# A PixArt-style block on one core: bias rows on GpSimd's queue, a LayerNorm moved into the stage before, and a new order in the last slots of self-attention

## The chip, the cores and the metric

The kernel runs on one core of a Trainium2 chip, in float32 throughout. A core has five engines with a queue each: TensorE (PE in the profile; its weight loads are listed as PEld), VectorE (DVE), ScalarE (ACT), GpSimd (POOL) and SyncE (SP). SP, ACT and POOL also issue transfers (DMAs) between the chip's main memory, called DRAM in the code, and the core's own memories SBUF and PSUM. An engine works through its queue in order; an instruction that waits holds up all that stand behind it on that engine. The metric is the device time of one execution in microseconds (us); lower is better.

## The reference

`x` is 8 sequences of 512 tokens with 512 channels, the context is 8 times 77 tokens, the condition one vector per sequence. There are 16 heads of 32 channels. Four stages follow each other, each adding to `x`:

```python
# 1 cross attention with adaptive LayerNorm on both sides ("x")
ada = lambda x, W, b: (1 + scale) * ln(x) + bias      # scale, bias = split(silu(c) @ W + b)
q  = ada(x, Wss_q, bss_q) @ Wq + bq
kv = ada(context, Wss_kv, bss_kv) @ Wkv + bkv
x  = x + softmax(q @ k.T / sqrt(32)) @ v @ Wp + bp
# six vectors for the later stages: shift_a, scale_a, gate_a, shift_m, scale_m, gate_m
mods = split(silu(c) @ W_mod + b_mod, 6)
# 2 self attention ("a")
x = x + gate_a * (attention((1 + scale_a) * ln(x) + shift_a) @ W_proj + b_proj)
# 3 cross attention with plain LayerNorm ("c")
x = x + (attention(ln(x) @ W_qc + b_qc, ln(context) @ W_kvc + b_kvc) @ W_cproj + b_cproj)
# 4 MLP ("m")
x = x + gate_m * (gelu(((1 + scale_m) * ln(x) + shift_m) @ W_mlp1 + b_mlp1) @ W_mlp2 + b_mlp2)
```

## The kernel before

The kernel works batch by batch (one sequence of 512 tokens as four tiles of 128) and stage by stage; between stages `x` goes through DRAM tensors `xa`, `xc`, `xm`. A batch's sequence is one SBUF tile of 1 MB, and three such tiles exist (`xres`). Weights pass through five SBUF tiles of 1 MB (`weights`).

**Setup (lines 228 to 262).** ACT's queue issues the loads of the condition (`c_sb`), of the context (`cx`, two transfers), and of nine bias vectors into the rows of one tile `brow` (line 237); then ACT computes `cs`, the Silu of the condition. PE transposes `brow` into `bcol`, which holds every bias as a column, and `cs` into `csT`. `mod_pair` (line 168) then computes scale and bias of the adaptive LayerNorm, for the context (`mod_kv`) and for `x` (`mod_q`): for each half it loads a weight, multiplies (line 175), copies the result out on ACT (line 180), transposes it back (line 183) and adds the bias on DVE (line 187).

**Context (`context_x`, line 401).** DVE normalises the five row tiles of the context, PE transposes them channel block by channel block (`cT_ps_x`, line 420), DVE multiplies by the scale (line 424) and adds the bias (line 428). Then come the values (line 394; they go through DRAM to be laid out by token) and the keys (line 442).

**Cross phase (`cross_phase`, line 528; used for x and c).** It runs over 32 units (batch b, head group fc). A unit has `scores` (PE line 561, then the softmax on DVE and ACT, lines 570 to 579), and `outputs` of the unit before (transposes line 597, copies on ACT, products line 602, `oT` on DVE line 609). In between, a queue of small generators (`Filler`) supplies matmuls: the queries of the next unit, the projection of the batch before (`project`, residual on DVE line 352 and POOL line 356, store line 357), and the LayerNorm of the next batch (`ln_T`, line 303): statistics on DVE (line 274), a reciprocal root in twelve small DVE steps (lines 286 to 295), `xh` (line 299), transposes (line 315). `next_x` loads the sequence of the next batch on ACT's queue at the first unit of each batch. The order of PE is the program's; DVE, ACT, POOL and SP are ordered by the compiler's list scheduler, which follows its own estimate of when each instruction is ready. `issue_after(ins)` forces what its block issues on the engine of `ins` to stand behind `ins` in that engine's queue; the dictionary `behind` hands such instructions to `ln_T`.

**Self phase (`self_phase`, line 650).** Here all five engines follow the order of the program. A group is one head group of one batch, and each slot of the loop (line 911) finishes group g and starts the next: scores of the next group (line 771) are copied to `e` on ACT (line 789) while DVE takes maxima (line 791); `maxima` and `spread` (lines 803, 806, 814, 820) write the row maxima to DRAM; `shift` (line 825) adds their negatives to `e` by eight accumulating transfers on POOL's queue; then come the exponentials (line 834), sums (line 841), outputs (line 854), the total (line 864) and the division (lines 871, 874). `beside` gives each slot its matmul work (values, queries, keys, projections). `later` keeps the residual additions and stores of projections, which `flush` issues. In the last batch, `ContextC` loads, normalises and transposes the context for stage c. After the loop the last group is finished together with the context's values (line 394) and keys (line 518): this is called the last slot. The slot (7,1) below is the one of batch 7, head group 1.

## Time and profile before

| what | value |
|---|---|
| time of the runs, median of 3 | 2706.99 us (2702.71 to 2710.66) |
| the profiled execution: its own time, and its span from first to last instruction | 2709.26 us, 2707.5 us |
| PE, DVE, ACT, POOL busy, share of the span | 95%, 62%, 39%, 30% |
| granted PE clock, mean over the span | 0.983 |
| first scores of stage x; last projection of stage x starts | 85.9 us; 494.5 us, 14 us long |
| first transposes of stage a; first scores of stage c | 515.5 us; 1499.3 us |
| last store of stage c's result | 1899.6 us |

In the profile, "L12" is line 12 of the kernel before. A timeline line has the start in us, the length in us, the engine, the line, the operation, output and inputs, shapes, a count, and in square brackets how long the engine was idle before and what released it. "ACTq" and "SPq" are the queues' own transfer issues. A line of the list of waits has the engine, its line, what it waited for, then the total in us, how often, and the longest. The first letters of a tile's name are sometimes cut by the profile, and the releaser of a wait on several transfers is the one that came last by its records.

### The profile page before, as it was taken

The page shows a single profiled execution, that of the slowest core. Times are in us where ns is not written, and L with a number is a line of the kernel's source. Part 1 is how long each engine was busy: PE and PEld are TensorE (multiplying, and loading weights), DVE is VectorE, ACT ScalarE, POOL GpSimd, SP SyncE. Part 2 cuts the span into 40 slices and gives each one's busy share as a digit, 9 for nine tenths or more (in the row PEclk, how much of TensorE's full clock was granted, in tenths as well). Part 3 has the DMA queues.
Part 4 walks back from the last instruction along what each step waited for, and adds up shares of the span by engine and source line. Part 5 has one row for each costly group of instructions (what it writes and reads, how often), then busy time and mean ns, then how long its engine had stood idle before and what let it go on. Part 6 is the DMA issues. An engine that isn't in the chain of part 4 may idle for free. (4 is left out here: it accounts for less than half of the span.)

```text
span 2707.5 us, 33555 instructions
## 1 busy us (share of the span) xinstructions
PE 2562.5 (95%) x13029; PEld 1498.7 (55%) x13029; DVE 1677.8 (62%) x2917; ACT 1058.7 (39%) x1466; POOL 822.0 (30%) x679
## 2 busy tenths in 40 slices
PE   6999999889999999999988999999999999999998
PEld 2555554433333333333333544454788888888887
DVE  4666666456776766767573767776755455465553
ACT  1433333256666666665752433333211211211210
POOL 0000001146766767667673001011411011011011
PEclk9989999999999999999999999999999999999999
DMA  6111121268988898998887111113110111110110
GB/s 243 40 51 51 48 82 52 82 125 176 178 182 184 180 186 168 195 184 175 178 194 209 58 36 43 47 40 105 51 35 29 39 36 34 34 35 34 34 36 24
DMA packets 114757, 264.95 MB, mean 98 GB/s; under 512 B 10418, under 2 KB 27406, under 8 KB 114598
## 3 DMA queue, kind: packets, MB, share of 16 engines
q0 software_dynamic: 36864, 134.23, 26.1%
q1 hardware_dynamic: 58037, 90.54, 10.0%
q10 hardware_dynamic: 19697, 38.03, 4.4%
q8 instruction: 103, 1.69, 0.2%
q14 instruction: 56, 0.46, 0.1%
HBM read 226.39 MB, written 36.37 MB: 97 GB/s over the span
## 5 line engine op out<-in xcount | busy, mean ns | idle before, releaser
L789 ACT COPY e_a<-sT_a 128x1024 f32<-128x1024 f32 x256 | 253.7, 1013 | 137.5 <-PE sT_a L771 109.9
L834 ACT ACTIVATE e_a<-e_a 128x1024 f32<-128x1024 f32 x256 | 262.7, 1056 | 49.8 <-DMA e_a<-mxd_a 47.1
L1244 POOL TENSOR_TENSOR res_m<-res_m,gate_m 128x256 f32<-128x256 f32 x64 | 52.1, 814 | 665.1 <-DVE res_m L1242 665.1
L825 POOL DMA_DIRECT2D e_a<-mxd_a x256 | 228.1, 2056 | 77.8 <-DMA mxd_a<-mxT_a 46.9
L791 DVE TENSOR_TENSOR mx_a<-sT_a,mx_a 128x1024 f32<-128x1024 f32 x128 | 152.8, 1220 | 123.9 <-PE sT_a L771 103.8
L841 POOL TENSOR_TENSOR sum_a<-e_a,e_a 128x1024 f32<-128x1024 f32 x64 | 152.4, 2400 | 195.1 <-ACT e_a L834 195.1
L1178 ACT ACTIVATE hT<-hT,bcol 128x512 f32<-128x512 f32 x128 | 91.9, 722 | 236.7 <-DVE hT L1153 228.6
L356 POOL TENSOR_TENSOR x_x<-x_x,res_x 128x512 f32<-128x512 f32 x32 | 40.5, 1266 | 468.8 <-DVE res_x L352 396.5
L771 PE MATMUL sT_a<-qT_a,kT_a 32*128 32x512 f32 x1024 | 149.2, 647 | 13.4 <-ACT e_a L789 12.6
L854 PE MATMUL o_ps_a<-e_a,v 128*32 128x512 f32 x1024 | 147.6, 617 | 11.4 <-ACT e_a L834 11.2
L841 POOL TENSOR_TENSOR sum_a<-sum_a,e_a 128x1024 f32<-128x1024 f32 x64 | 149.8, 2363 | 12.8 <-ACT e_a L834 12.5
L356 POOL TENSOR_TENSOR x_c<-x_c,res_c 128x512 f32<-128x512 f32 x32 | 40.6, 1270 | 369.2 <-DVE res_c L352 296.3
L598 ACT COPY pT_x<-pT_ps_x 77x512 f32<-77x512 f32 x128 | 73.0, 577 | 167.0 <-PE pT_ps_x L597 165.1
L329 PE MATMUL q_ps_x<-xnT_x,w_L_xcond_Wq 128*128 128x512 f32 x256 | 134.8, 613 | 0.0
L871 DVE RECIPROCAL rz_a<-z_ps_a 128x512 f32<-128x512 f32 x32 | 107.3, 3353 | 43.6 <-PE z_ps_a L864 43.6
L841 DVE TENSOR_TENSOR sum_a<-sum_a,e_a 128x1024 f32<-128x1024 f32 x64 | 86.3, 1379 | 75.4 <-ACT e_a L834 50.1
L1145 PE MATMUL q_ps_h<-x_m,w_L_xcond_W_mlp 128*128 128x256 f32 x512 | 132.3, 381 | 0.0
L329 PE MATMUL q_ps_c<-xnT_c,w_L_xcond_W_qc 128*128 128x512 f32 x256 | 131.6, 600 | 0.0
L1145 PE MATMUL q_ps_h<-xT_m,w_L_xcond_W_mlp 128*128 128x256 f32 x512 | 131.4, 379 | 0.0
L1145 PE MATMUL q_ps_h<-x_m,w_s 128*128 128x256 f32 x512 | 122.1, 382 | 5.6 <-DVE w_s L1099 4.6
L337 PE MATMUL proj_ps_x<-w_L_xcond_Wp,oT_x 128*128 128x512 f32 x256 | 123.4, 626 | 3.4 <-DVE oT_x L609 3.4
L598 ACT COPY pT_c<-pT_ps_c 77x512 f32<-77x512 f32 x128 | 72.3, 577 | 128.7 <-PE pT_ps_c L597 128.7
(236 smaller groups left out, 5110.0 us busy)
## 6 DMA issues: line engine op xcount, KB each, us to landing
e_a<-mxd_a POOLq DMA_DIRECT2D x256, 512.0 KB, 14.9
x_x<-in_x_dram ACTq DMA_DIRECT2D x8, 1024.0 KB, 5.0
xa<-x_x SPq DMA_DIRECT2D x32, 256.0 KB, 2.0
x_a<-xa ACTq DMA_DIRECT2D x8, 1024.0 KB
xr_a<-xa ACTq DMA_DIRECT2D x32, 256.0 KB, 7.7
xc<-xr_a SPq DMA_DIRECT2D x32, 256.0 KB, 2.1
x_c<-xc ACTq DMA_DIRECT2D x8, 1024.0 KB, 5.1
w_L_xcond_W_mlp<-in_L_xcond_W_mlp_dram SPq DMA_DIRECT2D x8, 1024.0 KB, 5.2
```

The lines of the kernel that those rows point to most:

```text
L329: nc.tensor.matmul(ps, lhsT=w[:, k, ts(j, P)], rhs=xT[k], start=(k == 0), stop=(k == KC - 1))
L337: nc.tensor.matmul(ps, lhsT=xT[k][:, cols], rhs=w[:, k, :], start=(k == 0), stop=(k == KC - 1))
L598: nc.scalar.copy(pTs[-1][:, h % 2, :], pp[:S, :])
L771: nc.tensor.matmul(sc[h // 2][:, h % 2, :], lhsT=kT[ts(h, HD), ts(k, P)], rhs=qT[ts(h, HD), :], start=True, stop=True,)
L789: nc.scalar.copy(self.e[k][i], sc[i])
L791: nc.vector.tensor_tensor(self.mx[1 - i], sc[1 - i], self.e[0][1 - i] if k == 1 else self.mx[1 - i], ALU.max,)
L825: nc.gpsimd.dma_start(out=self.e[k][i].rearrange("p h n -> p (h n)"), in_=self.mxd[2 * i : 2 * i + 2, :] .rearrange("h n -> (h n)").partit ...
L834: nc.scalar.activation(self.e[k][i], self.e[k][i], AF.Exp)
L841: engine.tensor_tensor(sum_i, self.e[0][i] if k == 1 else sum_i, self.e[k][i], ALU.add)
L854: nc.tensor.matmul(self.po[ts(h, HD), :], lhsT=vt[:, self.fc * P + h * HD : self.fc * P + (h + 1) * HD], rhs=self.e[k][h // 2][:, h % 2, : ...
L871: nc.vector.reciprocal(r, self.pz)
L1145: nc.tensor.matmul(self.banks[n][:, half], lhsT=lhsT, rhs=rhs, start=(k == 0), stop=(k == len(pairs) - 1),)
```

## The change

It has parts at four places.

1. *Setup and context.* The nine bias rows are issued by GpSimd's queue. `csT` is made before `bcol`. `mod_pair` becomes `mod_half`, which takes an already loaded weight and gives back its ACT copy; the two halves for the context stay in the setup, the two for `x` go into `context_x`, one after every second channel block. The weights are loaded in another order. The load of the first sequence is queued behind the last ACT copy of the context's modulation. The bias addition of the context (four times) moves from DVE to GpSimd. The PSUM pools `ps_s` and `ps_x` get the finer setting by which a tile waits only for the tiles of an earlier pool that it overlaps.
2. *Cross phases.* The statistics of batch 0 are queued on DVE behind the context's last multiplication (x) or, as before, behind the last division of self (c); those of batch 1 behind the softmax of unit (0,0), which held for c alone before; those of batch b+2 behind the softmax of unit (b,2). Each sequence's load is queued on ACT behind the last exponential of the unit before.
3. *From x to self.* The first LayerNorm of the self phase (`normalise_a(0)`) is written into the end of stage x, before the last `outputs`.
4. *The end of self.* All four shifts of a slot are written at its start, which leaves each engine's own order as it was. In batch 7, slot (7,1) has its queries and keys first and only one projection, slot (7,2) has three; the context for c is loaded in (7,1) instead of (7,2), and its LayerNorm is cut into other pieces, the reciprocal root after the `maxima`. In the last slot the copies of the context's values (evacuations) are issued one step later, after the next exponential and addition, and the loads of the first sequence of c and of the residual tiles go from ACT's queue to SP's.

```diff
-    def mod_pair(wname, bname, dst, pool, psp):
-        for u in range(2):
-            w = load_w(wname, u)
-            ps = psp.tile([P, H], F32, tag="ps", name=f"mod_ps_{wname}_{u}")
...
+    def mod_half(u, w, bname, dst, pool, psp, tag):
+        ps = psp.tile([P, H], F32, tag=tag, name=f"mod_ps_{bname}_{u}")
...
+        mark = nc.scalar.copy(m, ps[:B, :])
...
+        return mark
...
-    def next_x():
+    def next_x(queue=nc.scalar):
...
-            nc.scalar.dma_start(
+            nc.gpsimd.dma_start(
                 out=brow[at : at + n, :],
...
         nc.scalar.activation(cs, c_sb, AF.Silu)
+        cp = spp.tile([P, H], F32, tag="ps", name="csT_ps")
+        for k in range(KC):
+            nc.tensor.transpose(cp[:, ts(k, B)], cs[:, ts(k, P)], ident[:B, :B])
+        nc.vector.tensor_copy(csT.rearrange("p k b -> p (k b)"), cp[:, : KC * B])
         bp = spp.tile([P, H], F32, tag="ps", name="bcol_ps")
...
-        mod_pair("L0_xcond_Wss_kv", "L0_xcond_bss_kv", mod_kv, sp, spp)
-        w_l0 = [load_w("L0_xcond_Wkv", 0), load_w("L0_xcond_Wkv", 1)]
-        mod_pair("L0_xcond_Wss_q", "L0_xcond_bss_q", mod_q, sp, spp)
-        next_x()
+        w_ss_kv = [load_w("L0_xcond_Wss_kv", u) for u in range(2)]
+        for u in range(2):
+            mark = mod_half(u, w_ss_kv[u], "L0_xcond_bss_kv", mod_kv, sp, spp, "ps")
+        w_ss_q = [load_w("L0_xcond_Wss_q", 0)]
+        w_l0 = [None, load_w("L0_xcond_Wkv", 1)]
+        w_l0[0] = load_w("L0_xcond_Wkv", 0)
+        w_ss_q.append(load_w("L0_xcond_Wss_q", 1))
+        with tc.issue_after(mark.ins):
+            next_x()
...
+    def normalise_a(b):
+        xb = [x_sb["a", 0][:, t, :] for t in range(NT)]
+        mv, y = yield from ln_stats_pieces(xb, P, 1e-6, f"a{b}")
+        yield
+        for t in range(NT):
+            normalise(xb[t], xb[t], mv, y, t, P)
+            if t % 2:
+                yield
...
-    with tc.tile_pool(name="ps_s", bufs=2, space=PSUM) as ps_s:
+    with tc.tile_pool(name="ps_s", bufs=2, space=PSUM, reuse_waits="tile") as ps_s:
...
+            yield
             v = v()
             nc.scalar.copy(v[:n, :], pv[:n, :])
...
-                nc.vector.tensor_tensor(
+                last = nc.vector.tensor_tensor(
                     d, pt[:, :R].rearrange("p (b s) -> p b s", s=S),
...
-                nc.vector.tensor_tensor(
+                nc.gpsimd.tensor_tensor(
                     d, d, mod_kv[:, KC + k, :].unsqueeze(2).to_broadcast([P, B, S]), ALU.add
                 )
+                if k % 2:
+                    mark = mod_half(k // 2, w_ss_q[k // 2], "L0_xcond_bss_q", mod_q, prep, ps_m, "m")
...
-                    if t == CT // 2:
+                    if t in (2, CT - 1):
                         yield
                 y = rsqrt(mv[:, :, 1], 1e-6, "cc", CT)
...
-                    nc.scalar.activation(p, p, AF.Exp)
+                    behind["load"] = nc.scalar.activation(p, p, AF.Exp)
...
-                if behind:
+                if fc == 0:
                     behind.setdefault(1, last)
+                elif fc == 2:
+                    behind.setdefault(b + 2, last)
...
                         b, eps, nm, work, ps_m, st[b]["xT"], mod_q[:, 0:KC, :], mod_q[:, KC:, :],
+                        behind=behind.get(b),
...
                 if fc == 0:
-                    next_x()
+                    with tc.issue_after(behind["load"].ins):
+                        next_x()
...
+                elif fc == 1 and not more:
+                    todo = [queries(b, 3), keys(b, 3), project(b - 1, 0)]
+                elif fc == 2 and not more:
+                    todo = [project(b - 1, t) for t in (1, 2, 3)]
...
-            run(ln_pieces(0))
             for k in range(KC):
                 transpose_x(0, k)
...
+                for k in range(NT):
+                    g.shift(k)
+                flush(0)
                 flush(1)
...
-                if not more and fc == 2:
-                    ctx_c.load()
-                    ln = ctx_c.norm()
-                g.shift(0)
-                g.shift(1)
...
                 nxt.scores(1)
...
+                if fc == 2 and not more:
+                    next(ln, None)
                 g.exp(0)
                 pump(f[1], 4)
+                if fc == 1 and not more:
+                    ctx_c.load()
+                    ln = ctx_c.norm()
...
                 nxt.scores(3)
-                if fc == 2 and not more:
-                    next(ln, None)
...
                 nxt.maxima()
-                if fc == 0 and more:
+                if fc == 0 and more or fc == 2 and not more:
                     next(ln, None)
...
                 if fc == 2 and not more:
-                    next(ln, None)
+                    for _ in ln:
+                        pass
                 g.add_up(3)
...
+            value = None
             for k in range(NT):
                 g.exp(k)
                 if k:
                     g.add_up(k)
+                    run(value)
                 g.outputs(k)
+                if k == 2:
+                    next_x(nc.sync)
+                    for t in range(NT):
+                        load_tile(B - 1, t, nc.sync)
                 if k + 2 < CT:
-                    ctx_c.values(k + 2)
-                if k == 2:
-                    next_x()
-                    for t in range(NT):
-                        load_tile(B - 1, t)
+                    value = ctx_c.values(k + 2)
+                    next(value)
+            run(value)
...
             behind = {0: g.finish()}
-            run(ctx_c.keys(1))
+            behind["load"] = run(ctx_c.keys(1))
...
-            ps_m = stack.enter_context(tc.tile_pool(name="ps_x", bufs=2, space=PSUM))
+            ps_m = stack.enter_context(tc.tile_pool(name="ps_x", bufs=2, space=PSUM, reuse_waits="tile"))
...
             cross_phase(
-                "x", 1e-5, w_l0[2:], names, True, kT, vs, stack, between=later_modulation
+                "x", 1e-5, w_l0[2:], names, True, kT, vs, stack, behind={0: last, "load": mark},
+                between=later_modulation, ending=lambda: run(normalise_a(0)),
             )
```

## The prediction

> **What bounds the kernel now.** I read the page first, then TensorE's waits, then the timeline at the four places where the long waits lie. On the page TensorE (PE) is the bound: 95% busy, DVE 62%, ACT 39%. So only PE's idle stretches can be won, and each must be found by its place. The waits of PE, longest in total first:
>
> ```profile
> PE 2562.5 (95%) x13029; PEld 1498.7 (55%) x13029; DVE 1677.8 (62%) x2917; ACT 1058.7 (39%) x1466; POOL 822.0 (30%) x679
> ...
> PE bcol_ps L245 <- DMA row_L_xcond_b_mod<-in_L_xcond_b_mod_dram: 17.4, 1, 17.4
> ...
> PE o_ps_a L854 <- ACT e_a L834: 11.2, 15, 4.4
> ...
> PE mxT_ps_a L814 <- DVE nmx_a L806: 9.4, 2, 7.9
> PE lnT_ps_a L693 <- DVE x_a L299: 7.2, 2, 7.0
> PE o_ps_x L602 <- ACT pT_x L598: 6.4, 4, 2.1
> ```
>
> Four single waits stand out: 17.4 before the first matmul, 7.0 at a LayerNorm, 7.9 at the maxima, up to 4.4 at an exponential. The first, in the timeline:
>
> ```profile
> 3.67 0.31 ACTq L237 DMA_DIRECT2D brow<-in_L_xcond_bq_dram  x1
> 11.95 0.28 ACTq L237 DMA_DIRECT2D brow<-in_L_xcond_bkv_dram  x1
> 14.74 1.28 ACT L242 ACT_TABLE_LOAD   x1 [14.74 <-DMA brow<-in_L_xcond_b_kvc_dram]
> 17.36 0.39 PE L245 MATMUL bcol_ps<-ident,brow 92*128 92x92 f32 x1 [17.36 <-DMA row_L_xcond_b_mod<-in_L_xcond_b_mod_dram]
> 18.61 5.18 PE L175 MATMUL od_ps_L_xcond_Wss_kv<-w_L_xcond_Wss_kv,csT 128*8 128x512 f32 x8 [0.35 <-DVE csT L256]
> 40.62 1.28 PE L420 MATMUL cT_ps_x<-ident,cx 128*128 128x128 f32 x10 [0.90 <-DVE mod_q L187]
> 44.42 15.86 PE L394 MATMUL cv_ps_x<-w_L_xcond_Wkv,cT_x 128*128 128x512 f32 x35
> ```
>
> The nine bias loads sit on ACT's queue ahead of the Silu; the queue stands from 3.98 to 11.95, and PE starts at 17.36 instead of when weights are there. The context's values start at 44.42. The other three:
>
> ```profile
> 515.51 4.68 PE L693 MATMUL lnT_ps_a<-ident,x_a 128*128 128x128 f32 x16 [7.00 <-DVE x_a L299]
> 1417.38 0.38 PE L814 MATMUL mxT_ps_a<-ident,nmx_a 128*16 128x128 f32 x1 [7.86 <-DVE nmx_a L806]
> 1441.69 2.00 PE L854 MATMUL o_ps_a<-e_a,v 128*32 128x512 f32 x8 [1.68 <-ACT e_a L834]
> 1458.94 2.87 PE L854 MATMUL o_ps_a<-e_a,v 128*32 128x512 f32 x8 [4.38 <-ACT e_a L834]
> 1461.74 3.94 PE L518 MATMUL ckT_ps_c<-cT_c,w_L_xcond_W_kvc 128*128 128x512 f32 x8
> ```
>
> And one place where nothing waits yet, but DVE is full, the first cross batch:
>
> ```profile
> 97.73 1.50 DVE L579 TENSOR_TENSOR p_x<-p_x,sm_x 128x616 f32<-128x616 f32 x2
> 99.15 0.74 DVE L609 TENSOR_SCALAR oT_x<-o_ps_x,bcol 128x512 f32<-128x512 f32 x1
> 101.09 1.50 DVE L570 TENSOR_REDUCE mx_x<-s_x 128x8 f32<-128x616 f32 x2 [1.20 <-PE s_x L561]
> ```
>
> **The change, part by part** (minus is a gain).
>
> *Setup, −10.5.* With ACT's queue free, c_sb, cx and then the Silu follow: the last cx issue ends at 2.35, table load 1.28, Silu 0.63, transposes 0.59, copy 0.18, so csT at about 5. The first Wss_kv load landed 5.2 after its issue at 0.75. So the first product can start near 6 and take its 5.18; copy and transposes 1.0; the second 3.60 and 1.0: modulation of K/V done by about 17. Next bound is the context: cx landed at 11.95 beside the same transfers, and DVE went from there to the last normalise at 20.76; I keep that. From 20.8 PE goes in written order: two cT units 1.28, first mod_q half 3.60 with 1.0 for copy and transposes, two cT units 1.3, second half 4.6, together 11.8: values at 32.6, gain 11.8. Weights: Wss_kv, cx, Wss_q's first half and Wkv are 6.2 MB, the second half and x0 two more; at the 0.38 MB/us of the rows from 15 to 30 us that is landed by about 25, before it is due at 27. The rows on GpSimd have no like row in the trace. Low: nine issues at 0.89 (the shift's 7.12 for eight) after 1.3 of masks, 2.0 to land, as stores do: 11.3. High: the worst landing of a GpSimd transfer, 24.0: 33, values at about 46, a loss of 2. If they land at 14 and stand in front of the first product on PE, the chain is 14+10.8+11.8=36.6, gain 7.8. Small rows are nearest to the low end; between 11.8 and 7.8 I take 10.5.
>
> The Trainium skill ("DMA: Bandwidth & Descriptors", Issuing engines are not separate DMA queues) says that spreading transfers over engines saves only the sequencer's time, usually little. By that rule the move is worth nine issues of 0.31, some 2.8 us, and the whole sum would be −11.3; by the row ACT's queue stood 8 us between two issues, with the Silu behind.
>
> The four shift additions move to GpSimd: 1.27 for 512 columns there, so 1.5 for 616 against 0.75 on DVE. They hide behind the second mod_q half (4.6 on PE); without it the last would cost 1.5. The x0 load now waits for the modulation's copy on ACT (about 17), Wq and Wp behind it on SP; both are due only after values and keys (34 on PE): nothing. The pools' finer reuse waits remove at most the 0.90 at 40.62, counted in the chain.
>
> *LayerNorm of x1, +6.5.* Before, DVE did it in the idle setup (statistics at 28 to 38, normalise at 81.69). Now its statistics may issue only after the softmax of unit (0,0). That price: statistics 2.9, twelve small steps at 0.2, normalise 1.92: 7.2. In the first batch DVE is busy without a gap from 87.03 to 99.89, and PE's written order has x1's transposes (98.90) ahead of the scores of (0,2). If DVE serves the softmax of (0,1) first, x1 is ready at 99.89+7.2=107.1: PE loses 8.2. If the LayerNorm goes first, PE loses 1.4 at the transposes and 3.3 at the next probabilities: 4.7. The middle, 6.5.
>
> *LayerNorms of x2 and a0, +2.* x2 too was free in the setup; a0 comes new into batch 7. Four such LayerNorms already cost PE 6.4 (o_ps_x), 1.6 each. Two more: 0 to 3.2.
>
> *First LayerNorm of self, −6.5.* The wait of 7.00 goes; DVE has 7.7 of work for it and idles 14 us from 490 to 508 alone. If it lies before the last oT (494.62) it gives 3.2 back: −7.0 to −3.8. Late next: nothing; the transposes' inputs and W_proj (issued 478) are there.
>
> *Slots (7,1) and (7,2), −2.8.* Projects move: (7,1) loses one (3.7 on PE), (7,2) gains it. (7,1) wins next to nothing, because its end hangs on maxima, spread and the last exponential (1386.3); the cx load, 1.26 MB, now comes beside its shifts on full DMA engines: 0 to +3, say 1.5. On SP those five loads wait for the last key product (about 1373); behind them stands the maxima's store, due at 1385.4. In (7,2) the context's five-step statistics leave DVE's path before nmx (1409.5 to 1414.97), cx leaves the shifts; a third project fills PE where it waited 2.47. I step it through: maxima transposes 1407.4, nmx done 1410.8 instead of 1417.3, shift of the last group some 6 earlier, but the last addition waits for the eighth shift (1412) and the normalise: z done at 1418.5 instead of 1422.9, −4.3 (−2 to −6). GpSimd adds of a third project: 2.6 in a slot where it idled more.
>
> *Last slot, −7.7.* Exponential k+1 is queued ahead of evacuation k+2 on ACT, and five loads leave ACT for SP. The waits 1.68, 1.63 and 4.38 go, the first 1.63 stays. On SP the loads stand behind the value stores, which wait for ACT's copies; behind them stand the last value store and the load of all values, due only at the first c outputs (after 1510), and their own first reader is the c LayerNorm at 1471.6. Shifts take 25.8 until the last lands; if they bind, only 4.4 goes; at best all 9.3.
>
> The cross loops' later loads and the gates for b≥2 cost nothing: the load of x3 went out at 171.86, in (2,0), and is allowed there still.
>
> Sum: −10.5+6.5+2−6.5−2.8−7.7=−19.0. The profiled execution took 2709.26 (span 2707.5); it lies 2.3 above the median, so 2690.3 there is 2688 against 2706.99.
>
> **Rivals.**
> - *x1 costs nothing or the setup gives all:* with DVE's gaps enough, 2688−6.5=2681.5, with everything at its good end (−14 for a setup whose context lands earlier) near 2672. For: batch 0 has small gaps (1.20 at 101.09). Against: 7.2 does not fit them.
> - *The rows land late on GpSimd's queue:* setup gains 0 to 3, so 2696 to 2699; with the 33 of the high end 2700. For: 8 MB compete. Against: 46 KB in all.
> - *Slower: the LayerNorms slip a unit.* DVE is busy 30 to 38 us of 52 per batch. If gate and load put each statistic one unit later, PE waits in 13 batches at the lnT transposes; the nearest price is the c stage's, where a load stands before the exponentials (ACT waits 14.5 in 6) and PE pays (9.5+4.1)/6=2.3 a batch. At 1.5 a batch the gain is gone, at 2.3 it is 2688+30=2718. Against: the gates lie before the loads in time.
> - *No change that shows:* several parts at their poor ends, 2699 to 2707.
>
> **How the numbers follow.** Forecast 0.56 (2676 to 2698), better end 0.12, late rows 0.14 (half of it under 2699), slower 0.10, no change 0.08. About 0.3% (8.1 us) is what a measurement of this kernel can tell from no change. Faster 0.56+0.12+0.07=0.75, same 0.15, slower 0.10. The range 2672 to 2704 leaves out the slower case, half of the no-change case and a little below.
>
> **What would show it.** Right: the Silu near 4, the first product near 6 (not 18.61), values near 33; a PE wait of 5 to 8 at lnT_ps_x or pT_ps_x in the first batch; no gap before lnT_ps_a at the stage's start; mxT in the last batch waiting under 2; the c context's keys (1461.74) some 19 earlier. Wrong: bcol_ps still starting after 20, DVE idle behind GpSimd's additions, or waits of PE at lnT_ps_x and lnT_ps_c in every batch.

## The result, and the profile after

The kernel after the change takes 2716.78 us (median of 7 runs, 2713.97 to 2719.31); the kernel before, beside it, 2706.78 us (7 runs, 2702.5 to 2711.24). The ratio is 1.0038, with a 95% interval of 1.0025 to 1.0051: slower by some 10 us, where 19 us of gain were forecast. The profiled execution of after took 2715.6 us (span 2713.8), 6.3 us more than that of before in span; the other 4 us between the medians are the spread of single executions (the profiled one of before lay 2.5 above its median, that of after 1.2 below). The mean granted clocks are equal (0.984 and 0.983), so the two traces can be laid over each other, though the clock is not low at the same places in both.

I took the start of the same PE instruction in both traces, place after place. The difference "after minus before" steps up or down only where something was gained or lost; the steps are the ledger:

| stretch (the event at its end) | shift at its end, us | step, us | forecast of that part |
|---|---|---|---|
| setup (first scores of x: 85.86, 80.18) | -5.7 | -5.7 | -10.5 |
| x, batch 0, units (0,1) and (0,2) (scores of (0,3): 108.44, 112.47) | +4.0 | +9.7 | +6.5, x1's LayerNorm |
| x, batch 1, (1,0) and (1,1) (scores of (1,2): 138.96, 146.79) | +7.8 | +4.0 | part of +2, x2's |
| x, batches 2 to 6 (scores of (7,0)) | +6.0 | -1.8 | 0 |
| x, batch 7, (7,0) and (7,1) (scores of (7,2): 471.84, 482.91) | +11.1 | +5.1 | part of +2, a0's |
| x to self (first scores of self: 531.55, 534.83) | +3.3 | -7.8 | -6.5 |
| self up to slot (7,0) (a total z: 1363.63, 1366.29) | +2.7 | -0.6 | 0 |
| slots (7,1), (7,2) (first values of c's context: 1425.71, 1436.54) | +10.8 | +8.1 | -2.8 |
| last slot (first keys of c's context: 1461.74, 1461.00) | -0.7 | -11.5 | -7.7 |
| self to c (first scores of c: 1499.29, 1502.60) | +3.3 | +4.0 | 0 |
| c (first transposes of the MLP: 1897.15, 1903.36) | +6.2 | +2.9 | 0; +4.1 of it in (1,0), (1,1) |

Three gains came, one of them only by half. Six losses stand against them: one of them had a term of the other sign in the forecast (slots (7,1) and (7,2)), and two had none (the head of c, and c's batch 1). The page and the list of PE's waits of after (total, times, longest):

```profile
PE 2565.7 (95%) x13029; PEld 1493.2 (55%) x13029; DVE 1681.5 (62%) x2913; ACT 1058.4 (39%) x1466; POOL 833.6 (31%) x692
```

```profile
PE o_ps_x L622 <- ACT pT_x L618: 10.8, 5, 2.9
...
PE lnT_ps_c L318 <- DVE xh_c L302: 8.5, 4, 5.7
PE o_ps_a L865 <- ACT e_a L845: 8.3, 14, 2.1
PE bcol_ps L248 <- DMA brow<-in_L_xcond_b_mlp_dram: 7.5, 1, 7.5
PE z_ps_a L875 <- DVE sum_a L852: 6.7, 1, 6.7
PE lnT_ps_x L318 <- DVE xh_x L302: 6.2, 1, 6.2
PE proj_ps_x L340 <- DVE oT_x L629: 5.7, 2, 3.6
...
PE mxT_ps_a L825 <- DVE nmx_a L817: 4.7, 3, 1.6
```

The four single waits shown of before are gone or short: 7.0 at the transposes of self is away, 7.9 at the maxima is 1.6, 4.4 at an exponential is at most 2.1, 17.4 at the bias rows is 7.5. New single waits stand in their place: 6.2 at `xh_x`, 6.7 at `sum_a`, 5.7 at `xh_c`. In the timeline, the setup:

```profile
4.46 0.56 PE L244 MATMUL csT_ps<-ident,cs 8*128 8x8 f32 x4 [4.46 <-ACT cs L240]
...
12.51 0.41 PE L248 MATMUL bcol_ps<-ident,brow 92*128 92x92 f32 x1 [7.49 <-DMA brow<-in_L_xcond_b_mlp_dram]
12.69 2.47 DVE L426 BATCH_NORM_STATS2 cst_x<-cx 128x6 f32<-128x512 f32 x4 [12.69 <-DMA cx<-in_ctx_dram]
...
15.08 0.17 DVE L245 COPY csT<-csT_ps 128x32 f32<-128x32 f32 x1
...
15.31 6.25 PE L173 MATMUL od_ps_L_xcond_bss_kv<-w_L_xcond_Wss_kv,csT 128*8 128x512 f32 x8 [2.38 <-DVE csT L245]
```

The transposes of `csT` start at 4.46, as forecast; but the copy that lets PE go on runs on DVE only at 15.08, behind four statistics of the context, whose rows land at 12.69. Then the first cross batch:

```profile
99.11 1.92 DVE L302 TENSOR_SCALAR xh_x<-x_x,mv_x,lny_x 128x512 f32<-128x512 f32 x4
99.80 2.60 PE L318 MATMUL lnT_ps_x<-ident,xh_x 128*128 128x128 f32 x8 [6.19 <-DVE xh_x L302]
102.34 2.00 PE L579 MATMUL s_x<-ckT_x,qT_x 32*128 32x77 f32 x32
...
111.44 1.09 PE L318 MATMUL lnT_ps_x<-ident,xh_x 128*128 128x128 f32 x8
112.47 1.13 PE L579 MATMUL s_x<-ckT_x,qT_x 32*128 32x77 f32 x32
```

PE stands 6.19 for the LayerNorm of x1. Behind the wait its own work is slow as well: eight transposes take 2.60 us at 99.80 and 1.09 at 111.44, the scores of a unit 2.00 at 102.34 and 1.13 at 112.47. A view of stretches shows the granted clock there (start and end, length, then busy time and instructions of PE, PEld, DVE, ACT and POOL, then the clock):

```profile
99.80:102.40 2.60, 2.60 (x12) 1.51 (x12) 1.23 (x3) 0.78 (x1) 0.00 (x0) 0.50 0.00 0
102.40:106.60 4.20, 4.20 (x41) 3.28 (x41) 2.22 (x4) 0.58 (x1) 0.00 (x0) 0.57 0.02 4
```

From 106.60 to 110.00 it is 1.00 again. So of the 9.7 us of this stretch 6.2 are the wait, and the other 3.5 go with PE's own instructions, which took longer behind it. For x2's LayerNorm the loss lies at the output products of (1,0) and (1,1), first before, then after:

```profile
122.43 1.07 PE L602 MATMUL o_ps_x<-pT_x,cv_x 77*32 77x512 f32 x8
...
126.28 3.12 PE L622 MATMUL o_ps_x<-pT_x,cv_x 77*32 77x512 f32 x8
```

The second pair is 1.06 and 2.99 (133.46 and 139.37). The granted clock is 1.00 here; a row of several matmuls hides the pauses between them, so the list of waits shows none. And the places after it, up to the head of c (all of after):

```profile
520.44 1.09 PE L703 MATMUL lnT_ps_a<-ident,x_a 128*128 128x128 f32 x8 [0.85 <-DVE res_x L355]
...
1424.74 4.82 DVE L302 TENSOR_SCALAR cx<-cx,cmv_c,lny_cc 128x512 f32<-128x512 f32 x5
...
1430.74 3.06 PE L875 MATMUL z_ps_a<-sum_a,ones 128*32 128x512 f32 x8 [6.68 <-DVE sum_a L852]
...
1483.95 1.26 POOL L754 TENSOR_TENSOR res_a<-res_a,gate_a 128x512 f32<-128x512 f32 x1 [26.71 <-DMA gate_a<-gate_a]
...
1490.67 0.48 PE L318 MATMUL lnT_ps_c<-ident,xh_c 128*128 128x128 f32 x1 [5.70 <-DVE xh_c L302]
```

### The profile page after: what moved, and what is told of

Same layout as the page of the kernel before. It is cut to its first block, busy times and chain, and to the rows that moved or that the text cites. A ratio compares the mean times of both kernels' runs of the same rounds, so it can differ in the third digit from the quotient of the medians.

```text
span 2713.8 us, 33571 instructions
## 1 busy us (share of the span) xinstructions
PE 2565.7 (95%) x13029; PEld 1493.2 (55%) x13029; DVE 1681.5 (62%) x2913; ACT 1058.4 (39%) x1466; POOL 833.6 (31%) x692
## 4 chain that ended last, share of the span: by engine, by line
issue 27%; PE 23%; DMA 13%; POOL 7%; DVE 5%; ACT 3%; POOLq 0%; SPq 0%; ACTq 0%; DVEq 0%
DMA e_a<-mxd_a 9%; PE proj_ps_a L340 3%; PE proj_ps_c L340 3%; PE sT_a L782 3%; PE q_ps_a L332 2%; POOL res_m L1264 2%; PE k_ps_a L332 2%; POOL xr L1265 2%; PE q_ps_c L332 2%; PE mT_a L814 1%; ACT e_a L845 1%; POOL e_a L836 1%; PE o_ps_a L865 1%; DMA x_c<-xc 1%; DMA gate_m<-gate_m 1%
## 5 line engine op out<-in xcount | busy, mean ns | idle before, releaser
L852 POOL TENSOR_TENSOR sum_a<-sum_a,e_a 128x1024 f32<-128x1024 f32 x64 | 149.7, 2359 | 10.7 <-ACT e_a L845 9.9
L332 PE MATMUL q_ps_a<-xnT_a,w_L_xcond_W_qkv 128*128 128x512 f32 x256 | 122.3, 622 | 1.4 <-ACT xnT_a L705 1.4
```

What stands on the lines that cost most here:

```text
L332: nc.tensor.matmul(ps, lhsT=w[:, k, ts(j, P)], rhs=xT[k], start=(k == 0), stop=(k == KC - 1))
L852: engine.tensor_tensor(sum_i, self.e[0][i] if k == 1 else sum_i, self.e[k][i], ALU.add)
```

## The experiments

The theory after the two traces: each part has its own cost or gain at its own place, and these add up; the losses come from work that was put in front of something on a queue (VectorE twice, SyncE once) or into a full stretch. The rivals: another part is behind a loss than the one that stands next to it; or each gain is only taken back by the next thing that is late. Each run is compared at the same events, with the kernel it was made from or with the one that is named; "the run's span" is that of its profiled execution. The kernel before was timed beside them each time (medians 2703.5 to 2709.2), and ratios are against it.

### The statistics held behind a softmax

```diff
-                if fc == 0:
+                if fc == 0 and nm == "c":
                     behind.setdefault(1, last)
-                elif fc == 2:
-                    behind.setdefault(b + 2, last)
```

> Edit: the changed kernel, but the statistics of the next batch's LayerNorm are held behind no softmax any more, except batch 1 of the second cross attention, which was held so before the change as well. Theory (the holds put about 9.5 us of VectorE work into a phase in which VectorE is the engine that is waited for): the first units (0,1) and (0,2) of the first cross phase lose 9.5 us, units (1,0) and (1,1) 4 us, and the second cross phase 4 us in its units (0,2) to (1,1); span near 2696 us against 2713.8. Rival (the holds only move the same work about, and the later batches are set by something else, such as the load held behind an exponential): under 3 us in each place, span 2708 or more.

Measured: 2705.28 us, ratio 0.9983 (0.9969 to 0.9998), span 2704.2. The scores of (0,2) come 8.1 us sooner, (0,3) another 1.6: 9.7, as the theory has it. The LayerNorm of x1 now lies in DVE's idle stretch before the first scores:

```profile
46.07 1.29 DVE L277 BATCH_NORM_STATS2 st_x<-x_x 128x6 f32<-128x512 f32 x2 [6.58 <-DMA x_x<-in_x_dram]
...
74.44 1.92 DVE L302 TENSOR_SCALAR xh_x<-x_x,mv_x,lny_x 128x512 f32<-128x512 f32 x4 [21.46 <-PE lnT_ps_x L318]
```

But in (1,0) and (1,1), and in the second cross phase, nothing changed (0.1 us at most). That half of the expectation failed: the 4 us of x2 and of c's batch 2 have another holder.

### The loads held behind an exponential

```diff
                 if fc == 0:
-                    with tc.issue_after(behind["load"].ins):
-                        next_x()
+                    next_x()
```

> Edit: the changed kernel, but the load of the next batch's x in the cross phases is not held behind an exponential. Theory of the LayerNorm holds: nothing changes, span within 2 us of 2713.8, PE still waits about 6 us for xh_x in the first batch. Rival (the held load is what makes x late): the 6.2 us wait of PE for xh_x goes and the span falls by 8 us or more, to about 2705.

Measured: 2711.31 us, ratio 1.0007 (0.9994 to 1.002), span 2709.7. PE's 6.2 us for `xh_x` stay, and (0,1) is unchanged: the load is not what makes x1 late. (The next unit, (0,2), took 1.6 us longer than in after: in the first batch 13.7 us ran at a granted clock of 0.50, 10.2 in after. Three runs without this edit, a0_in_self, cst_first and cx_in_72, show the same.) But (1,0) and (1,1) are 1.1 and 1.9 us shorter, and the same two units of the second cross phase are together 3.0 us shorter: 3 of the 4 us at each place. In before, x2's load was issued at 23.84 and its LayerNorm done in the idle setup; in after the load is issued at 116.89, lands when batch 1 runs, and the LayerNorm falls into batch 1's full DVE. The load's hold alone is enough for the 4 us: with the statistics free and the load held nothing was won. With the load free and the statistics held, 1.0 of them is left; the run at the end, free of both, has these units as in before.

### Self's first LayerNorm back at the head of self

```diff
             first = groups[0]
+            run(normalise_a(0))
...
-                between=later_modulation, ending=lambda: run(normalise_a(0)),
+                between=later_modulation, ending=None,
```

> Edit: the changed kernel, but self's first LayerNorm stands at the head of self again, as before the change. Theory (moved work costs in the last cross batch what it saves at the boundary): units (7,0) and (7,1) get 5 us shorter, the stretch from the last product of the first cross phase to the first transposes of self about 6.5 us longer; span 2714 to 2716, that is +1.5 with 1.5 either side. Rival (as I predicted: it was hidden in the last batch at about 2 us): span 2717.5 to 2719.

Measured: 2717.77 us, ratio 1.0034 (1.0022 to 1.0046), span 2716.4, 2.6 more than after. Units (7,0) and (7,1) are 2.4 and 2.7 us shorter, 5.1 together, and the first transposes of self wait again:

```profile
500.10 14.00 PE L340 MATMUL proj_ps_x<-w_L_xcond_Wp,oT_x 128*128 128x512 f32 x32
521.11 4.26 PE L703 MATMUL lnT_ps_a<-ident,x_a 128*128 128x128 f32 x14 [7.01 <-DVE x_a L302]
```

Counted from the scores of (7,3), the first scores of self come 8.9 us later. So the move gains 8.9 at the boundary and costs 5.1 in the batch it was moved into; 3.8 are left by these places, 2.6 in the span. The span, 2716.4, lies between the two expectations; the places decide for the theory. In after the rows show the cost in batch 7 at the projection (PE waits 2.10 for `oT_x` at 468.09) and at the output products (1.21 for `pT_x` at 477.82).

### The copy of csT, and the bias rows

```diff
-        nc.vector.tensor_copy(csT.rearrange("p k b -> p (k b)"), cp[:, : KC * B])
+        csT_copy = nc.vector.tensor_copy(csT.rearrange("p k b -> p (k b)"), cp[:, : KC * B])
...
-                nc.vector.bn_stats(bn[:n], cx[:n, t, :])
-                nc.vector.bn_aggr(mv[:n, t, :], bn[:n])
+                with tc.issue_after(csT_copy.ins):
+                    nc.vector.bn_stats(bn[:n], cx[:n, t, :])
+                    nc.vector.bn_aggr(mv[:n, t, :], bn[:n])
```

> Edit: the changed kernel, but the context's statistics on VectorE are held behind the copy of csT, so that the copy does not stand behind statistics that wait for the context rows. Theory (the setup gained 5.7 us where 10.5 were predicted because of that place in VectorE's queue): first modulation product near 6 us instead of 15.3, values near 34, first scores 4 to 5 us earlier, span near 2709. Rival (the first products are set by the weights of the modulation or by the rows on GpSimd's queue): the products start early but the second and third still wait, first scores under 1.5 us earlier, span 2712 to 2714.

Measured: 2714.65 us, ratio 1.0019 (1.0008 to 1.0029), span 2711.1; first scores 2.45 us earlier than after, between the two expectations. The copy is at 5.05, and yet the first product starts at 12.91:

```profile
5.05 0.19 DVE L245 COPY csT<-csT_ps 128x32 f32<-128x32 f32 x1 [5.05 <-PE csT_ps L244]
...
12.56 0.41 PE L248 MATMUL bcol_ps<-ident,brow 92*128 92x92 f32 x1 [7.55 <-DMA row_L_xcond_b_mod<-in_L_xcond_b_mod_dram]
12.91 6.18 PE L173 MATMUL od_ps_L_xcond_bss_kv<-w_L_xcond_Wss_kv,csT 128*8 128x512 f32 x8
```

A second thing stood in front, on PE itself: the transpose of the bias rows, which land at 12.5. The next run moves it behind the first product:

```diff
+        if then is not None:
+            with tc.issue_after(product.ins):
+                then()
         m = pool.tile([B, H], F32, tag="mod", bufs=2, name=f"mod_{bname}_{u}")
...
+        def bias_columns():
+            bp = spp.tile([P, H], F32, tag="ps", name="bcol_ps")
+            nc.tensor.transpose(bp[:, :n_cols], brow, ident[:n_cols, :n_cols])
...
+                then=None if u else bias_columns,
```

> Edit: the changed kernel, with the copy of csT ahead of the context's statistics on VectorE, and the transpose of the bias rows behind the first modulation product on TensorE. Theory (the first product stood behind two things, the statistics and then the bias rows that land at 12.5): first product at 5.5 to 9, cT_ps_x near 21 (bound by the context's normalisation, which ends near 20.8) against 27.5, first scores 5 to 6.5 us earlier than the changed kernel's 80.18; span 2707.5 to 2709. Rival (the weights are late: four megabytes share the queues at the start): first product after 11, first scores no earlier than in the run with the copy alone, 77.7.

Measured: 2713.45 us, ratio 1.0024 (1.0011 to 1.0037), span 2711.1; first scores at 77.38, only 0.35 better than with the copy alone. The product starts at 6.36, so the weights are not late, but a third thing is:

```profile
6.36 6.09 PE L173 MATMUL od_ps_L_xcond_bss_kv<-w_L_xcond_Wss_kv,csT 128*8 128x512 f32 x8 [1.34 <-DMA w_L_xcond_Wss_kv<-in_L_xcond_Wss_kv_dram]
...
17.41 0.56 PE L183 MATMUL dT_ps_L_xcond_bss_kv<-ident,mod_L_xcond_bss_kv 8*128 8x8 f32 x4 [4.31 <-DVE lnt_cx L302]
17.90 5.45 PE L173 MATMUL od_ps_L_xcond_bss_kv<-w_L_xcond_Wss_kv,csT 128*8 128x512 f32 x8
```

The setup's PSUM pool has two buffers, and the next transposes wait for DVE, where the copy of the bias columns has its place behind the first steps of the context's reciprocal root. With four buffers (the run with everything, below) they start at 12.75.

### Slots (7,1) and (7,2) as before

The diff leads back to the order before at seven places; its core:

```diff
-                elif fc == 1 and not more:
-                    todo = [queries(b, 3), keys(b, 3), project(b - 1, 0)]
-                elif fc == 2 and not more:
-                    todo = [project(b - 1, t) for t in (1, 2, 3)]
...
+                if not more and fc == 2:
+                    ctx_c.load()
+                    ln = ctx_c.norm()
...
-                if fc == 1 and not more:
-                    ctx_c.load()
-                    ln = ctx_c.norm()
```

> Edit: the changed kernel, but in self's last batch the slots (7,1) and (7,2) have the order of before: the context's rows are loaded at the head of (7,2), two projections in each slot, the context's normalisation in its old pieces. The last slot keeps the new order. Theory (loading the context beside the shifts of (7,1), and normalising it in front of the last sums of (7,2), costs 8 us): slot (7,1) 5 to 6 us shorter, (7,2) 2 us shorter, PE's 6.7 us wait for sum_a gone, and 2 to 3 us of it lost again where the last slot waits for mxT; span 2706 to 2709 against 2713.8. Rival (the slots are longer because all four shifts go out together, which this edit leaves): (7,1) stays within 2 us of the changed kernel, span 2712 or more.

Measured: 2710.98 us, ratio 1.0014 (1.0002 to 1.0027), span 2703.4. Slot (7,1) is 5.9 us shorter, (7,2) 1.3; counted to the first values of c's context, and less the 3.2 by which this execution was ahead at the start of (7,1), the old order is 8.3 us better. PE waits 8.0 for the maxima again and no longer for `sum_a`.

Which of the moved things does it? The next run takes back the load and the pieces of the normalisation, and leaves the projections as the change has them (without the first four lines of the diff above):

```diff
+                if not more and fc == 2:
+                    ctx_c.load()
+                    ln = ctx_c.norm()
...
-                if fc == 1 and not more:
-                    ctx_c.load()
-                    ln = ctx_c.norm()
```

> Edit: the changed kernel, with the context's loads and the old pieces of its normalisation back in slot (7,2), but one projection in (7,1) and three in (7,2) as the change has them. Theory (the 1.2 MB of context rows beside the eight shifts of (7,1) delay the exponentials): (7,1) 5 to 6 us shorter than the changed kernel's 32.0, as in the run with both slots as before; (7,2) then costs 1 to 3 us more than in that run, for the third projection. Rival (the regrouped projections make (7,1) long): (7,1) within 1.5 us of the changed kernel.

Measured: 2719.47 us, ratio 1.0034 (1.0021 to 1.0048), span 2720.3. Slot (7,1) has its old length again, 6.0 us shorter than in after: the context's rows beside the eight shifts are the cause there. The median of the eight shifts of (7,1) took 16.3 us to land in after, 14.3 in this run and in before, and 13.8 in the run with the whole old order, and the last three exponentials of the slot wait for them in after:

```profile
1386.88 1.06 ACT L845 ACTIVATE e_a<-e_a 128x1024 f32<-128x1024 f32 x1 [2.04 <-DMA e_a<-mxd_a]
...
1390.04 1.06 ACT L845 ACTIVATE e_a<-e_a 128x1024 f32<-128x1024 f32 x1 [1.95 <-DMA e_a<-mxd_a]
1393.24 1.06 ACT L845 ACTIVATE e_a<-e_a 128x1024 f32<-128x1024 f32 x1 [2.14 <-DMA e_a<-mxd_a]
```

Slot (7,2), however, grew by 11.4 us against before, far more than the 1 to 3 expected. The chain, all of this run:

```profile
1400.69 0.33 SPq L758 DMA_DIRECT2D xc<-xr_a  x1
1401.07 5.43 SPq L485 DMA_DIRECT2D cx<-in_ctx_dram  x5
...
1413.57 0.69 DVE L493 BATCH_NORM_STATS2 cst_c<-cx 128x6 f32<-128x512 f32 x1 [7.45 <-DMA cx<-in_ctx_dram]
...
1421.29 1.01 ACT L800 COPY e_a<-sT_a 128x1024 f32<-128x1024 f32 x1 [11.83 <-DVE mx_a L802]
...
1422.36 3.67 PE L814 MATMUL mT_a<-ident,mx_a 128*128 128x128 f32 x16 [12.15 <-ACT e_a L800]
```

The one projection of (7,1) comes so late in the slot that its residual is added at the head of (7,2); its store waits for that on SP's queue, the five loads wait behind the store (issued 7.9 us after the first matmul of the total of (7,1); in the run with the whole old order 3.0 us before it, so 10.9 us later), and DVE's statistics, which stand ahead of the last maxima, wait for the loads. So the two moves belong together: with the projections regrouped the load has to go early, and early it lies beside the shifts.

### The gate's row first

```diff
-                if t == 0:
+                if t == 0 and "g" not in st[b]:
                     st[b]["g"] = gate_rows(gate_a, b, work, "a")
...
             value = None
+            st[B - 1]["g"] = gate_rows(gate_a, B - 1, work, "a")
             for k in range(NT):
                 g.exp(k)
```

> Edit: the changed kernel, but the gate's row for the last projections of self is loaded at the start of the last slot, and not behind the loads of x and of the residual tiles on SyncE's queue. Theory (the gate landed 16 us after its issue, at 1484, GpSimd's adds stood 26.7 us for it, and with them the residual on VectorE and the normalisation of c's first batch): PE's wait of 5.7 us for xh_c goes back to about 1.3, first scores of the second cross phase 4 us earlier, span near 2709.5. Rival (the residual tiles themselves land late, being behind x's load on the same queue): GpSimd then waits for xr_a instead and the gain is under 1.5 us.

Measured: 2710.63 us, ratio 1.001 (0.9995 to 1.0024), span 2708.5. The first scores of c come 4.4 us earlier from the total of the last slot on, and PE's longest wait for `xh_c` is 1.3 again. GpSimd no longer waits for a transfer:

```profile
1476.52 1.26 POOL L754 TENSOR_TENSOR res_a<-res_a,gate_a 128x512 f32<-128x512 f32 x1 [19.12 <-DVE res_a L751]
```

### The last slot alone, on the kernel before

```diff
                 if k:
                     g.add_up(k)
+                    run(value)
                 g.outputs(k)
+                if k == 2:
+                    next_x(nc.sync)
+                    for t in range(NT):
+                        load_tile(B - 1, t, nc.sync)
                 if k + 2 < CT:
-                    ctx_c.values(k + 2)
-                if k == 2:
-                    next_x()
-                    for t in range(NT):
-                        load_tile(B - 1, t)
+                    value = ctx_c.values(k + 2)
+                    next(value)
+            run(value)
```

> Edit: the kernel before, with the last slot alone in the new order (exponentials ahead of the evacuations of the values, loads of x and of the residual tiles on SyncE's queue). Theory (the parts add up place by place): from the first value product of c's context to the keys 11 us less, then 4 us given back at the head of the second cross phase, where the gate's row is late; span 2700 to 2701 against 2707.5. Rival (the last slot gains only because the slots ahead of it took over work, the loads and the projections): under 5 us less to the keys, span 2705 or more.

Measured: 2703.58 us, ratio 0.9978 (0.9965 to 0.9991), span 2694.3 (of which 5.5 are drift that this execution was ahead by before the edit begins). From z of slot (7,2) to the last z it gains 11.5, then gives back 3.7 at the head of c, where GpSimd waits 26.11 for the gate's row. Both are as in the change, to a few tenths. Which of the two pieces, the order of the exponentials or the queue of the loads, brings how much of the 11.5 was not tried. The 7.8 that are left lie inside what the ratio allows (2.4 to 9.5 us).

### All located costs taken out

The statistics free in x; loads held in the first batch of each cross phase alone; the copy, the first product and four PSUM buffers as above; the old (7,1) and (7,2); the gate's row first. What is new in it:

```diff
-    with tc.tile_pool(name="setup_ps", bufs=2, space=PSUM) as spp:
+    with tc.tile_pool(name="setup_ps", bufs=4, space=PSUM) as spp:
...
-                    with tc.issue_after(behind["load"].ins):
+                    with tc.issue_after(behind["load"].ins) if b == 0 else nullcontext():
                         next_x()
```

> Edit: the changed kernel with every cost taken out that the runs so far located: no statistics held behind a softmax in the first cross phase; the loads of x held behind an exponential in the first batch of each cross phase alone, so that batch 2's x lands in the idle stretch before the first scores; the copy of csT and the first modulation product in front, the bias rows' transpose behind it with four PSUM buffers in the setup; slots (7,1) and (7,2) as before; the gate's row first. Theory (the costs and gains are each bound to their place and add up): against the kernel before, first scores 11 us earlier (near 75), batches 0 to 6 unchanged, batch 7 +5, boundary to self -8, last slot -11, nothing given back at the second cross phase: span near 2682.5, 2679 to 2687. Rival (each boundary's gain is taken back by the next thing that is late, as it was in four places of the changed kernel): less than half of it, span 2695 or more.

Measured: 2681.43 us, ratio 0.9901 (0.9888 to 0.9914), span 2676.8: 30.7 us below the profiled execution of before, 27.8 below in the medians. It beats both kernels. Against before: first scores -10.7; unchanged up to the scores of (1,2), to a tenth; from there to the end of batch 6 -3.7; batch 7 +5.5; x to self -7.8; self up to the last slot -2.1; the last slot -11.6 to the keys; from there to c's first scores -0.8, so nothing is given back at its head; c itself unchanged (-0.2). The setup of this run:

```profile
6.16 5.81 PE L173 MATMUL od_ps_L_xcond_bss_kv<-w_L_xcond_Wss_kv,csT 128*8 128x512 f32 x8 [1.15 <-DMA w_L_xcond_Wss_kv<-in_L_xcond_Wss_kv_dram]
12.52 0.30 PE L252 MATMUL bcol_ps<-ident,brow 92*128 92x92 f32 x1 [0.55 <-DMA brow<-in_L_xcond_b_mlp_dram]
12.75 0.41 PE L183 MATMUL dT_ps_L_xcond_bss_kv<-ident,mod_L_xcond_bss_kv 8*128 8x8 f32 x4
...
20.97 2.32 PE L442 MATMUL cT_ps_x<-ident,cx 128*128 128x128 f32 x10 [3.20 <-DVE mod_kv L187]
```

The context's transposes start at 20.97: the bound that the forecast took from the context's normalisation (20.8), for PE waits there for `mod_kv`, which has its place behind that normalisation on DVE. The sum came 5.7 us better than expected in the profiled execution and 2.8 in the medians; that surplus lies in stretches where the code is as before (batches 2 to 6 of x, the batches of self), which differ by up to 5 us between two executions here, and I don't claim it.

### One piece of the change's (7,2) put back

The reciprocal root of the context's LayerNorm behind the maxima's reduction, once alone and once with the last sums ahead of the normalisation:

```diff
-                if fc == 0 and more:
+                if fc == 0 and more or fc == 2 and not more:
                     next(ln, None)
                 pump(f[3], 2)
...
-                if fc == 2 and not more:
-                    next(ln, None)
                 g.add_up(3)
+                if fc == 2 and not more:
+                    next(ln, None)
```

> Edit: the kernel with all located costs taken out, and from the change's order of slot (7,2) one thing back: the reciprocal root of the context's LayerNorm stands behind the maxima's reduction on VectorE instead of ahead of it. In the kernel it starts from, twelve small steps stand there from 1390.2 to 1396.1, and PE waits 7.93 for nmx. Theory (my forecast of -4.3 for (7,2) holds when the context's rows are loaded early and the third projection is away): PE's wait for nmx falls to 2 to 3, the maxima reach DRAM 5 us earlier, the last sums are delayed behind the root and the normalisation as before, and the last slot's first exponential runs 3 to 5 us earlier; the context's values start 1 to 4 us earlier than 1406.9. Rival (the root only changes its place: the sums that z needs stand behind root and normalisation together, so z and all that follows come no earlier): values within 1 us of 1406.9.

> Edit: as the run with the root behind the maxima, and the last sums (add_up of the fourth key tile) ahead of the normalisation on VectorE. Theory (z waits for these sums, and the normalisation of five tiles, 2.4 to 4.8 us, is what stands ahead of them): PE reaches z 2 us earlier than with the root alone, waits 1 to 2 us at the context's transposes instead, in sum 0 to 2 us more gained. Rival (GpSimd's additions slow the normalisation wherever it stands, and the transposes wait for all that was won): no gain, values start at the same time as with the root alone or later.

Measured: 2680.74 us (ratio 0.9909, 0.9887 to 0.9931) and 2680.69 us (0.9912, 0.9884 to 0.9939), four runs each; without, 2681.43 in five runs that lie 7 us apart, so medians can't tell 3 us here. The slot itself can. With the root moved, the values of c's context start at 1407.25, against 1406.94; with the sums moved too, at 1407.99, but that execution was 4.5 us behind when the slot began, in code that is the same in all three. Counted from the total of (7,1), z comes after 31.2 us without, 30.3 with the root moved and 26.6 with the sums moved too; the values after 35.9, 35.9 and 32.5. With the root moved the wait of 7.93 for the maxima is gone and PE waits for `sum_a` instead (2.29):

```profile
1398.24 1.05 PE L870 MATMUL o_ps_a<-e_a,v 128*32 128x512 f32 x4 [1.50 <-ACT e_a L850]
1401.59 2.94 PE L880 MATMUL z_ps_a<-sum_a,ones 128*32 128x512 f32 x8 [2.29 <-DVE sum_a L857]
```

With the sums ahead of the normalisation as well, z follows them without a listed wait:

```profile
1400.88 2.36 DVE L857 TENSOR_TENSOR sum_a<-sum_a,e_a 128x1024 f32<-128x1024 f32 x2
...
1402.17 3.06 PE L880 MATMUL z_ps_a<-sum_a,ones 128*32 128x512 f32 x8
...
1403.16 2.41 DVE L308 TENSOR_SCALAR cx<-cx,cmv_c,lny_cc 128x512 f32<-128x512 f32 x5
```

For the first run the rival is right: the root only changes its place, and the sums stand behind root and normalisation. In the second the theory is right, and the gain is larger than its 0 to 2: z comes 4.6 us sooner than without both moves, 1.1 of it is lost again at the context's transposes, and 3.5 are left at the values. The four executions with the old order of (7,2) (before, old_7, last_slot_alone and the run above) need 35.9 to 36.1 us for this stretch, so 3.5 is clear of their scatter; still, each of the two new orders was profiled once.

## Why the prediction was wrong

*What bounds the kernel.* Right in the main: most losses and gains are idle stretches of PE, found by their places. What the forecast left out is PE's own work behind a long wait. Behind waits of 4.4, 7.0 and 7.9 us in before (1458.94, 515.51, 1417.38) and of 6.2 and 5.7 in after (99.80, 1490.67) the granted clock was 0.50, and the instructions there took up to about twice as long. A sum of waits alone is too small there.

*Setup, -10.5: measured -5.7.* The failing step is "csT at about 5 ... so the first product can start near 6". The transposes were at 4.46 and the weights there at 6.16 to 6.36, but I put the copy on DVE without asking what DVE's list has in front of it: four statistics waiting for rows that land at 12.69. The low bound of the row "if they land at 14 and stand in front of the first product" (7.8) names the second obstacle, which showed once the first was away. Without both, and with PSUM buffers enough, the term is -10.7, with the context's normalisation as the bound, as the working had it. Values started at 39.25 instead of 33. The rows themselves landed by 12.5, so the rival of late rows is out. That this is near the low bound of 11.3 is partly luck: the bound took 0.89 for each issue and 2.0 for the landing, and the rows took 0.50 to 0.72 and 5.4 to 6.8. The four additions on GpSimd took 1.2 each (2.39 for two) and were hidden.

ACT's table load moved from 14.74 to 2.40: what stood behind the bias rows on the issuing queue came 12 us sooner, and the -10.7 of the finished run rests on that together with the new order of the setup; the rows' move alone was not run. The rule weighed there, of the Trainium skill ("DMA: Bandwidth & Descriptors", Issuing engines are not separate DMA queues), is that spreading issues over engines saves only the sequencer's time, usually little. By it the move would have been worth an estimated 2.8 us, and the 12 us of the table load don't agree with that.

*LayerNorm of x1, +6.5: measured +9.7*, beyond my upper bound of 8.2. The mechanism is right (x_no_ln_gates takes away 9.7, and PE's wait at `lnT_ps_x` was 6.2, in the 5 to 8 named as its sign). Mis-sized: my terms were waits alone, and PE's other 3.5 us are its work behind the wait, at a granted clock of 0.50 and 0.57. The eight executions that keep the hold all show the loss: from the scores of (0,0) to those of (0,3) they need 9.7 to 11.4 us more than before, and the four longest, from 11.1 on, are those with 13.7 us at 0.50 instead of 10.2.

*LayerNorms of x2 and a0, +2: measured +4.0 and +5.1.* The step "1.6 each" is the error: I divided the listed waits of PE at `o_ps_x` by four LayerNorms. x2's 4.0 lie at these same products, 2 us in each of two units, but as pauses inside a row that the list does not count; ACT's copies for the products (126.65) stand there behind an exponential that waited 2.52 us for DVE (126.03). a0 costs at the projection too (`oT_x`). In these two batches a LayerNorm cost 4.0 and 5.1.

*"The cross loops' later loads and the gates for b≥2 cost nothing":* wrong twice. I looked at x3, whose load is bound by the three tiles of `xres` anyway; the load that mattered was x2's, which went out at 23.84 before and at 116.89 after. The same in c, +4.1, which the forecast had left out.

*First LayerNorm of self, -6.5: measured -7.8 at the boundary*, 8.9 by the run that puts it back. Right: the wait of 7.00 fell to 0.85. The other 1.65 are the transposes and what follows them, at a granted clock of 0.50 behind the wait in before (515.50 to 520.20) and of 1.00 in after (520.40 to 525.00).

*Slots (7,1) and (7,2), -2.8: measured +8.1.* For the load beside the shifts I took 1.5 between 0 and 3; it is 6.0 in after and 4.1 to 6.1 in all executions that have it there. My step said that the slot's end hangs on the last exponential, and still gave the load no more than 3: three exponentials in a row waited 2 us each, and the products behind the third ran at a granted clock of 0.50 (1392.90 to 1398.20). For (7,2) the -4.3 came from letting the statistics leave the path of the maxima. The last two runs show what was missing: without the load and the third projection the root's new place alone gains nothing, since the last sums stand behind root and normalisation and PE waits for them; with the sums ahead of the normalisation 3.5 of the 4.3 appear. My step noted that "the last addition waits for the eighth shift (1412) and the normalise", and then still counted the gain.

*Last slot, -7.7: measured -11.5*, the upper bound was 9.3. That the gain belongs to this slot is shown by the run on the kernel before. The bound was too low since it counted waits alone: the products behind the three waits took 2.00, 2.00 and 2.87 us in before (the last at a granted clock of 0.50) and 1.06 to 1.07 in after; with that difference the 7.7 us of waits come to 11.4. The keys start at 1461.00 in after where the sign asked for some 19 us less than 1461.74, because the parts ahead, forecast at -11.3 together, had come to +10.8.

*The gate's row, not in the forecast: +4.0.* I followed the five loads to SP's queue and named two transfers behind them, the last value store and the load of all values. A third one, the gate's row that `project` issues, was behind them as well, and it had the nearest reader. The run with the row first gives back 4.4.

*The rivals.* The slower case came true in sign, but not by its mechanism: there are no waits at the transposes in every batch; PE's list has one in x (6.2) and four in c (8.5, of which 5.7 is the gate's row). The losses in x lie in three batches whose LayerNorm had been done in idle time or in another stage before.

## What to carry to other kernels

A step that starts earlier starts only as early as the slowest queue it crosses: follow it through every engine's list, including the small copies, and through the PSUM buffers, and expect the second and third obstacle behind the first. Work in an idle stretch was free here; the same 7.2 us of DVE work in a full stretch cost PE 4 to 5 us, and 9.7 in the first batch. So before an order is imposed on LayerNorms or loads, look where the old order had put them. When a long wait of PE is priced, look at PE's rows behind it too: here they ran at half the granted clock. When transfers change queue, list everything that stands behind them there, and look at the one with the nearest reader; when transfers change slot, look at what the slot's end waits for.

## What the runs showed of the hardware that I had not expected

*Small DVE operations can stand for a whole GpSimd addition.* In the run with everything, the two first steps of the context's reciprocal root, 128x5 values each and 0.17 us elsewhere, took 1.79 and 2.26:

```profile
1389.65 4.65 POOL L857 TENSOR_TENSOR sum_a<-sum_a,e_a 128x1024 f32<-128x1024 f32 x2
...
1390.24 1.79 DVE L295 TENSOR_SCALAR lnv_cc<-cmv_c 128x5 f32<-128x5 f32 x1
1392.07 2.26 DVE L297 TENSOR_SCALAR lny_cc<-lnv_cc 128x5 int32<-128x5 int32 x1
1394.36 0.17 DVE L300 TENSOR_SCALAR lnv_cc<-lnv_cc 128x5 f32<-128x5 f32 x1
```

They end at 1392.03 and 1394.33; two GpSimd additions, 4.65 together, end at 1391.98 and at 1394.30. The other way round, in after a GpSimd product of 128x512, 1.26 elsewhere, took 5.37 from 1427.56 on, beside DVE's normalisation, which itself took 4.82 where 2.37 is usual. (GpSimd was still issuing shifts until 1430.5 there, so which of the two held DVE up is not shown.) The Trainium skill ("SBUF — State Buffer", SBUF: two separate sides) describes the ports that the two engines share as an exclusive lock for the whole instruction; the ends of the first rows agree with that.

*PE is slow when it begins, and behind a long wait.* The same eight matmuls of a modulation took 6.25 us at 15.31 in after, 6.09 at 6.36 and 5.45 after a gap of 4.31 in setup_fixed, and 3.60 when PE had just been busy. Behind that gap the granted clock was 0.50 (17.80 to 21.00) and then 0.86 (21.00 to 23.40). At the program's start the profile gives 1.00, but its first record of the clock in after comes at 20.67, so this is no measurement; the matmuls there follow each other 0.85 us apart, as they do at 0.50 behind the gap, and 0.43 apart at 1.00. The Trainium skill ("TensorE: Matmul & The Clock Gate", What's actually happening) has the array at half rate for about its first 3.4 us of work; by that, as an estimate, the eight would take 5.3; the 5.45 and the clock beside it agree.

*A drift of up to 6 us* adds up between the profiled executions of different kernels in stretches with the same code (-5.5 in last_slot_alone before its edit begins, +4.5 in combo_root_add against combo). Steps of one place mostly repeat to some tenths (x2's 3.9 to 4.2 us), those at the halved clock to 1.7 (x1's 9.7 to 11.4); a sum over hundreds of microseconds can't be read so. So places have to be compared from an event shortly ahead of them.
